# Splitting a group norm's last aggregate, moving its chain, and a new ending for a window-attention and convolution kernel

## The chip, the cores and the metric

One core of a Trainium2 chip runs the whole program. The metric is the device time of one execution in microseconds, the median of several runs. The engines are named as in the profile: PE (TensorE matmul), PEld (its weight loads), DVE (VectorE), ACT (ScalarE), POOL (GpSimd) and SP (SyncE, which here only issues DMAs). Each engine works through its own queue of instructions in order and waits for the others by semaphores.

## The reference

The input `x` is 2 images of 128 channels x 256 x 256, fp32. Two layers follow, each a residual around a group norm (32 groups of 4 channels, statistics over the whole image).

```python
# layer 0: windows of 8x8 queries, keys and values from 12x12 around them, 4 heads of 32
x = x + L0(_gn(x))
    qkv = einsum('bchw,oc->bohw', x, W_qkv)
    attn = q*SCALE @ k.T + rel_pos_emb(q) + FIXED_MASK   # mask: only every second row and column
    out = softmax(attn) @ v                              # then W_out
# layer 1: three convolutions, no activation
x = x + L1(_gn(x))
    t1 = conv(x, w1)          # 5x1 along the height, 128 -> 128 channels
    t3 = conv(t1, w3)         # 3x1 along the height, depthwise
    t4 = unfold3_dil2(x) * w4 # 3 taps of distance 2 along the width, 128 -> 8 channels
    y  = t4 * t3              # the 8 channels repeated 16 times
```

The mask leaves only pairs of pixels whose row and column offsets have one parity, so a window splits into four classes (row parity, column parity) of 16 queries and 36 keys.

## The kernel before

Channels lie on the 128 partitions. An image is cut into 32 strips of 8 rows, `k` counts the 64 strips of both images (`NB` = 2, `NS` = 32). Two generator-like stages run one after the other and overlap a little at their border.

**Set-up** (L226 to L254). 32 loads of 8 rows (1 MB) of image 0 go through six buffers, and `Norms.chunk` (L117) makes one `bn_stats` of 512 columns for every two rows: 128 in all. Then `Norms.steps` (L123) is run to its end inside `normalise(0)`: one `bn_aggr` over all 768 statistics (L127), a matmul with an averaging matrix that puts the mean over 4 channels (L130), mean and variance on DVE, a second such matmul (L141), square root on ACT (L147), and five small DVE operations for the reciprocal and one for the negated mean.

**Layer 0** (`attention_fast`, from L165). The order on every engine is the program's order (`manual_schedule`), so each call below stands in the queues of all engines at the place where it is written. The unit `u` is half a strip (a row parity `r`); there are 128. In a unit: at `r == 0` the next strip is normalised (`normalise`, DVE L322, L327, L328 and POOL L313); `input_stats` makes four `bn_stats` of the second image while the first is worked on, mostly in odd units and in units 4 and 8; `by_place` (POOL L337) sorts the next strip's pixels; `biases` (L458) and `scores` (L474) fill the four PSUM banks `s0` to `s3`; ACT takes the exponential (L483); `values` (L439) makes four PSUM tiles that ACT and DVE copy out half each (L445); `coefficients` (L418) for the next strip; `attend` (L499) with its division on DVE (L505, L506); `turn`, the transposes on DVE (L517); keys (L354) in even units, queries (L393) in odd ones; `result_stats`, two `bn_stats` of the unit before; `project` (L354, DVE L533), which adds the residual and stores x1 to DRAM (SP L537). All PSUM tiles but the scores' come from one ring of four banks, `ps_pj`: a tile's matmul waits until the tile four before it has been read.

The group norm of the second image (`x1`) is spread over unit 61, that of the first image's result (`y0`) over unit 69: `norm_at` names the unit and the seven calls of `step()` in the loop each run one piece of `Norms.steps`. The norm of the second image's result (`y1`) is run in pieces in strips 3 to 7 of layer 1. In unit 8 DVE forms the six sums of convolution weights (`Weights.sums`, L641 to L644).

**Layer 1** (`convolutions_fast`, a generator). Its first pieces (loads, normalisation, row sums, unfold of strip 0) are called by `next(layer1)` in the last units of layer 0. Then per strip: `unfold(k)` (four matmuls L740, two ACT copies L750 and L751, five small DMAs L754 that shift pixels), `first_rows(k)`, two calls of `vertical` (the 5x1 convolution with shared sums: matmuls L760 and L799, ACT copy L794, DVE L803, L810, L816, and ACT L821, the first tap of the 3x1 convolution), `depthwise` (the other two taps, DVE L828), `spread` (four matmuls L839 that repeat the 8 channels) into the score banks, and `combine` (DVE L849), the product. `finish` adds the residual by a DMA of POOL that accumulates (L857), and one strip later `store` writes the result. The last strip adds the residual itself, half on POOL (L870, L871), half on DVE (L873), and stores in two halves.

Tiles come from pools whose memory is a stack: the pools of layer 1 (`f_t1`, `f_wk1`) are opened after those of layer 0 are closed and reuse their memory; `f_both`, `f_raw` and the PSUM pools live through both layers.

Of the kernel before, what the change touches and what calls it, by code (L numbers as in the profile page):

```python
# [20 lines left out]
P = 128  # L21
W = 256
# [84 lines left out]
class Norms:  # L107


    def __init__(self, nc, glob, small, gavg, ns):  # L110
        self.nc, self.glob, self.small, self.gavg, self.ns = nc, glob, small, gavg, ns
        self.done = {}

# [8 lines left out]

    def steps(self, st, ps_pool, name, tag="pj"):  # L123

        nc, glob, small, gavg = self.nc, self.glob, self.small, self.gavg
        mv = small.tile([P, 2], F32, tag="mv", name=f"mv_{name}")
        nc.vector.bn_aggr(mv, st.rearrange("p n k -> p (n k)"))  # L127
        yield
        pm = ps_pool.tile([P, 512], F32, tag=tag, name=f"pm_{name}")
        nc.tensor.matmul(pm[:, 0:1], gavg, mv[:, 0:1], start=True, stop=True)  # L130
        yield
        mean = glob.tile([P, 1], F32, tag=f"mean_{name}", name=f"mean_{name}")
        nc.vector.tensor_copy(mean, pm[:, 0:1])
        d = small.tile([P, 1], F32, tag="d", name=f"d_{name}")
        nc.vector.tensor_sub(d, mv[:, 0:1], mean)
        q = small.tile([P, 1], F32, tag="q", name=f"q_{name}")
        nc.vector.tensor_mul(q, d, d)
        nc.vector.tensor_add(q, q, mv[:, 1:2])
        yield
        pv = ps_pool.tile([P, 512], F32, tag=tag, name=f"pv_{name}")  # L140
        nc.tensor.matmul(pv[:, 0:1], gavg, q, start=True, stop=True)  # L141
        yield
        v = small.tile([P, 1], F32, tag="v", name=f"v_{name}")
        nc.vector.tensor_scalar(v, pv[:, 0:1], 1e-5, None, ALU.add)
# [23 lines left out]
def attention_fast(tc, io, x1_d, norm, st_x, st_y, tags, ends, weights, both, layer1):  # L168
# [6 lines left out]
    with ExitStack() as l0:  # L175
# [49 lines left out]
        with ExitStack() as setup:  # L225
# [35 lines left out]

        stats_at, norm_at = {}, {}
        for b in range(NB - 1):
            for s in range(NS - 2):
                stats_at[2 * (b * NS + s) + 1] = b + 1, s
            stats_at[2 * (b * NS + 2)] = b + 1, NS - 1
            stats_at[2 * (b * NS + 4)] = b + 1, NS - 2
            norm_at[2 * (b * NS + NS - 2) + 1] = st_x, b + 1, f"x{b + 1}"
            norm_at[2 * ((b + 1) * NS + 2) + 1] = st_y, b, f"y{b}"
        coming, sxs = sorted(stats_at), {}  # L270

        def load_next():
            if coming:
                u = coming.pop(0)
                b, s = stats_at[u]
                sxs[u] = t = rawp.tile([P, 8, W], F32, tag="sx", name=f"f_sx_{b}_{s}", bufs=1)
                nc.sync.dma_start(t, x[b, :, 8 * s : 8 * s + 8, :])

        def input_stats(u):
            b, s = stats_at[u]  # L280
            norm.chunk(st_x[b], 4 * s, sxs.pop(u))

# [270 lines left out]
        with tc.manual_schedule(engines=ORDERED):  # L553
# [7 lines left out]
            for u in range(NU):  # L561
# [35 lines left out]
                attend(u)  # L597
                step()
                if not later:
# [23 lines left out]
class Weights:  # L623
# [14 lines left out]
    def sums(self):  # L638

        w = [self.w1[:, i] for i in range(5)]  # L640
        self.nc.vector.tensor_add(self.w1s[:, 0], w[1], w[3])  # L641
        self.nc.vector.tensor_scalar(self.w1s[:, 1], w[3], -1.0, None, ALU.mult)
        for i, (a, b) in enumerate(((2, 1), (4, 3), (0, 1), (2, 3))):
            self.nc.vector.tensor_sub(self.w1s[:, 2 + i], w[a], w[b])  # L644


def convolutions_fast(tc, io, x1_d, norm, st_y, out, weights, count_good, both):
# [4 lines left out]
    with ExitStack() as l1:  # L652
# [11 lines left out]
        def load_rows1(b, s):  # L664

            if s == 0:
                pre = rawp.tile([P, 8, W], F32, tag="sx", name=f"raw1_{b}_pre", bufs=1)
                nc.sync.dma_start(pre[:, 5:8, :], x1_d[b][0][:, 0:3, :])
# [66 lines left out]
        def unfold(k):  # L735
# [26 lines left out]

        def first_rows(k):

            s = k % NS
            xt = xn[k % 2]
            t3 = wk.tile([P, 8, W], F32, tag="t3", name=f"t3_{k}")
# [4 lines left out]
            if s == 0:  # L772
                nc.gpsimd.memset(t1[:, 0:1, :], 0.0)
                top = taps(
                    f"{k}_first", 1,
                    [(w1[:, tap], xt[:, tap - 1 : tap, 2 : 2 + W]) for tap in (2, 3, 4)],
                )
                nc.scalar.copy(t1[:, 1:2, :], top)
            else:
                nc.scalar.copy(t1[:, 0:2, :], t1s[k - 1][:, 8:10, :])  # L780
            if s + 1 == NS:
                nc.gpsimd.memset(t1[:, 9:10, :], 0.0)

        def vertical(k, m, between=None):
# [13 lines left out]
            for i, w in enumerate((w1[:, 1], w1s[:, 1])):  # L798
# [18 lines left out]
                t1[:, 2 * m - 1 : 2 * m + 2 * n - 2 : 2, :], pa[:, 0:n], c[:, 0:n], ALU.add  # L817
            )
            t3 = ts[k][1]
            j = 2 * m - 4  # L820
# [43 lines left out]

        def finish_half(k, half):

            b, s = divmod(k, NS)
            t4, t3, y = ts[k]
            if half == 0:
                nc.gpsimd.tensor_tensor(y[:, 0:3, :], y[:, 0:3, :], raws[b, s - 1][:, 5:8, :], ALU.add)  # L870
                nc.gpsimd.tensor_tensor(y[:, 3:4, :], y[:, 3:4, :], raws[b, s][:, 0:1, :], ALU.add)  # L871
            else:
                nc.vector.tensor_tensor(y[:, 4:8, :], y[:, 4:8, :], raws[b, s][:, 1:5, :], ALU.add)  # L873
            nc.sync.dma_start(
                out[b, :, 8 * s + 4 * half : 8 * s + 4 * half + 4, :], y[:, 4 * half : 4 * half + 4]
            )

# [8 lines left out]
        yield  # L886
        unfold(0)
        yield

        tp = l1.enter_context(tc.tile_pool(name="f_t1", bufs=2))  # L890
        wk = l1.enter_context(tc.tile_pool(name="f_wk1", bufs=2))
        with tc.manual_schedule(engines=ORDERED):
            rows_buffer(1)
            for k in range(NB * NS):
                more = k + 1 < NB * NS
                if k + 2 < NB * NS:
                    load_rows1(*divmod(k + 2, NS))
                if k > 0:
                    unfold(k)
                first_rows(k)  # L900

# [18 lines left out]
                if not more:  # L920
                    finish_half(k, 0)
                depthwise(k, 4)
                combine(k, banks, (2, 3))
                if more:
                    finish(k)
                else:
                    finish_half(k, 1)

# [614 lines left out]
```

## Time and profile before

| what | value |
|---|---|
| three runs | 3078.32, 3076.55, 3078.05 us; median 3078.05 |
| the profiled execution | 3077.89 us, of it 3076.0 us span |
| mean granted TensorE clock | 0.998 |
| PE busy | 2950.9 us (96%) |
| DVE busy | 2522.4 us (82%) |
| ACT busy | 1732.8 us (56%) |
| POOL busy | 657.8 us (21%) |
| HBM read, written | 284.59 MB, 134.22 MB |

The span is the time from the first to the last instruction of the profiled execution; the runs' times hold also what lies around it. In lines of the timeline the columns are the start in us, the duration, engine, line, operation, output and inputs, how many instructions are merged into the line, and in brackets the engine's idle time ahead of it with what ended it. In lines of waits they are the waiting engine and line, what it waited for, the total in us, how often, and the longest.

### The profile page before, as it was taken

The numbers are of one execution on the slowest core, as the hardware profiler recorded it, in microseconds if no ns is written. First come the engines' busy times: TensorE is split into PE (matmuls) and PEld (weight loads), VectorE is DVE, ScalarE is ACT, GpSimd is POOL, SyncE is SP. The second block draws the span as 40 slices with busy tenths as digits, with TensorE's granted clock in tenths as the row PEclk, the third lists the DMA queues.
The fourth block names the chain that finished last, engine by engine and source line by source line (L and its number), as shares of the span: only waits on it lengthen the run. The fifth ranks groups of instructions, "written<-read, shape, count | busy, mean of one in ns | idle before, by whom it ended". The sixth has DMA issues, their size and how long they took to land.

```text
span 3076.0 us, 116627 instructions
## 1 busy us (share of the span) xinstructions
PE 2950.9 (96%) x52090; PEld 2223.8 (72%) x52090; DVE 2522.4 (82%) x4092; ACT 1732.8 (56%) x2673; POOL 657.8 (21%) x1433
## 2 busy tenths in 40 slices
PE   0799999999999999999999999999999999999998
PEld 0688888888888888888888888884444444444443
DVE  8788888888888877777777777768999999999998
ACT  0455555555555655555555555555666665666664
POOL 2322232323232222323232323220000000000001
PEclk9999999999999999999999999999999999999999
DMA  9433333333333221222222222225788888888886
GB/s 393 167 126 126 114 117 113 116 113 116 112 117 113 85 72 65 89 72 90 73 90 73 90 72 89 73 96 141 209 222 221 215 210 217 216 217 216 217 216 167
DMA packets 137404, 434.78 MB, mean 141 GB/s; under 512 B 12992, under 2 KB 87616, under 8 KB 104384
## 3 DMA queue, kind: packets, MB, share of 16 engines
q1 hardware_dynamic: 127824, 361.18, 33.8%
q0 software_dynamic: 9072, 66.06, 11.7%
q8 instruction: 412, 6.75, 0.9%
q14 instruction: 96, 0.79, 0.1%
HBM read 284.59 MB, written 134.22 MB: 136 GB/s over the span
## 4 chain that ended last, share of the span: by engine, by line
PE 93%; DVE 2%; ACT 1%; issue 0%; POOL 0%; DMA 0%; SPq 0%; DVEq 0%; ACTq 0%
PE f_pv L439 15%; PE a_e L760 10%; PE a_o L760 10%; PE f_s L474 8%; PE f_o L499 8%; PE f_pk L354 8%; PE f_pq L393 7%; PE f_py L354 7%; PE f_pa L418 4%; PE f_s L458 4%; PE a_d L799 3%; PE b L839 2%; PE a_c L760 2%; PE g L740 2%; POOL f_xq L337 0%
## 5 line engine op out<-in xcount | busy, mean ns | idle before, releaser
L445 DVE COPY f_vt<-f_pv 64x512 f32<-64x512 f32 x512 | 354.2, 695 | 299.5 <-ACT f_vt L445 299.3
L337 POOL COPY f_xq<-f_xn 128x128 f32<-128x128 f32 x1024 | 399.2, 441 | 707.9 <-DVE f_xn L322 647.9
L439 PE MATMUL f_pv<-f_wqkvT,f_xn 128*128 128x128 f32 x4096 | 491.3, 278 | 0.0
L439 PEld LDWEIGHTS f_pv<-f_wqkvT,f_xn 128*128 128x128 f32 x4096 | 466.9, 192 | 8.6
L483 ACT ACTIVATE f_p<-f_s 128x512 f32<-128x512 f32 x512 | 264.5, 602 | 320.0 <-PE f_s L474 320.0
L399 ACT ACTIVATE f_q<-f_pq,f_head 128x512 f32<-128x512 f32 x512 | 303.1, 703 | 145.2 <-PE f_pq L393 145.2
L445 ACT COPY f_vt<-f_pv 64x512 f32<-64x512 f32 x512 | 298.2, 584 | 116.9 <-PE f_pv L439 116.5
L821 ACT ACTIVATE t<-t,w 128x1024 f32<-128x1024 f32 x128 | 146.9, 1148 | 372.4 <-DVE t L816 367.9
L828 DVE SCALAR_TENSOR_TENSOR t<-t,w,t 128x1024 f32<-128x1024 f32 x256 | 329.9, 1288 | 7.4 <-ACT t L821 1.3
L474 PEld LDWEIGHTS f_s<-f_q,f_kt 64*64 64x64 f32 x16384 | 250.9, 135 | 50.1 <-issue 49.9
L474 PE MATMUL f_s<-f_q,f_kt 64*64 64x64 f32 x16384 | 268.7, 220 | 0.6 <-issue 0.6
L367 ACT COPY f_kt<-f_pk 128x512 f32<-128x512 f32 x256 | 154.6, 604 | 196.4 <-PE f_pk L354 196.4
L499 PE MATMUL f_o<-f_vt,f_p 128*32 128x66 f32 x16384 | 263.6, 222 | 1.4 <-issue 0.7
L857 POOL DMA_DIRECT2D y<-f_x x63 | 54.7, 868 | 915.2 <-DVE y L849 900.2
L499 PEld LDWEIGHTS f_o<-f_vt,f_p 128*32 128x32 f32 x16384 | 241.9, 110 | 10.8 <-DVE f_cf L431 1.0
L354 PE MATMUL f_py<-f_ot,f_woT 128*128 128x256 f32 x1024 | 242.2, 379 | 2.2 <-DVE f_ot L517 2.2
L354 PE MATMUL f_pk<-f_xn,f_wqkvT 128*128 128x256 f32 (+2 forms) x1258 | 243.0, 345 | 0.0
L393 PE MATMUL f_pq<-f_xq,f_wq_s 128*128 128x256 f32 (+1 forms) x1370 | 240.5, 331 | 0.8 <-DVE f_rc L505 0.8
L313 POOL COPY f_xn<-f_xn 128x1280 f32<-128x1280 f32 x62 | 86.7, 1399 | 720.6 <-PE f_pv L439 720.6
L760 PE MATMUL a_e<-xm,w1s 128*128 128x512 f32 x512 | 240.7, 591 | 0.0
L760 PE MATMUL a_o<-xm,w1s 128*128 128x512 f32 x512 | 240.3, 590 | 0.0
L393 PEld LDWEIGHTS f_pq<-f_xq,f_wq_s 128*128 128x128 f32 x1370 | 208.2, 191 | 23.3 <-PE pv_x L141 0.4
(131 smaller groups left out, 4696.9 us busy)
## 6 DMA issues: line engine op xcount, KB each, us to landing
f_raw<-in_x SPq DMA_DIRECT2D x62, 1280.0 KB, 7.8
f_sx<-in_x SPq DMA_DIRECT2D x64, 1024.0 KB, 12.4
f_x<-f_x SPq DMA_DIRECT2D x128, 512.0 KB, 3.4
y<-f_x POOLq DMA_DIRECT2D x63, 1024.0 KB, 8.0
out<-y SPq DMA_DIRECT2D x63, 1024.0 KB, 4.4
raw<-f_x SPq DMA_DIRECT2D x64, 640.0 KB, 6.4
raw<-f_x SPq DMA_DIRECT2D x62, 384.0 KB, 6.5
t<-t4p SPq DMA_DIRECT2D x192, 32.0 KB, 4.7
```

The costliest lines, as they stand in the source:

```text
L337: nc.gpsimd.tensor_copy(xq[:, half, t2, :, :, c].rearrange("p t r n e -> p r t n e"), cells[:, :, 16 * half + c : 16 * half + 16 : 2, 1 + ...
L354: nc.tensor.matmul(dst[:, 512 * lo // last : 512 * hi // last], w, moving[:, n * lo // last : n * hi // last], start=True, stop=True,)
L367: nc.scalar.copy(cur[:, c, 1:129, 2:6], pk.rearrange("p (j i) -> p j i", i=4))
L393: nc.tensor.matmul(pq.rearrange("p (h n e t) -> p h t n e", h=2, n=8, e=2)[:, half, lo:hi], wq_s, xq[:, half, :, :, r, c].rearrange("p s t ...
L399: nc.scalar.activation(q[:, c, :, i], pq.rearrange("p (n x) -> p n x", n=NPAIR), AF.Copy, scale=head[:, i : i + 1],)
L439: nc.tensor.matmul(pv[:, P * n : P * n + P], xn[k % 2][:, r, 4 * j + n].rearrange("p c x -> p (c x)"), wvT, start=True, stop=True,)
L445: (nc.vector.tensor_copy if c else nc.scalar.copy)(vt[rows, 4 * j : 4 * j + 4, :, c, 0:32], pv[rows].rearrange("p (n h d) -> p n h d", n=4 ...
L474: nc.tensor.matmul(sc[g][n // 8][64 * c : 64 * c + 64, n % 8].rearrange("p i x -> p (i x)"), keys_k[rows, c, 48 * n : 48 * n + 64], qs[u][ ...
L483: nc.scalar.activation(pts[u][:, g, 8 * half : 8 * half + 8].rearrange("p n i x -> p (n i x)"), sc[g][half].rearrange("p n i x -> p (n i x ...
L499: nc.tensor.matmul(po[32 * h : 32 * h + 32, n - lo], p[:, h // 2, n, h % 2], vt[:, n, h], start=True, stop=True,)
L760: nc.tensor.matmul(pa[:, : n * W], w, rows, start=i == 0, stop=i == len(terms) - 1)
L828: nc.vector.scalar_tensor_tensor(t3[:, j : j + 4], t1[:, j + tap : j + tap + 4, :], w3[:, tap : tap + 1], t3[:, j : j + 4], ALU.mult, ALU.add,
```

## The change

- **Aggregate in quarters.** A new `quarter` runs `bn_aggr` over a quarter of the statistics; `steps` takes the four means and variances and combines them (with `last=True` it makes the fourth quarter itself, with `last=False` all four have been made). In the set-up the quarters stand between the loads; for `x1`, `y0` and `y1` they are placed at the end of chosen even units (`quarter_at`).
- **Statistics of the second image.** 30 loads in odd units only: eight of 10 rows, then 22 of 8 rows. Units 4 and 8 have none.
- **Chain of the norm.** The `step()` calls move within units 61 and 69: two after `scores`, two after `values`, one ahead of `attend`, one after `turn`.
- **Weight sums** on POOL instead of DVE.
- **Keys** of the second image's first strip, part 0: one matmul of 512 columns instead of two of 256.
- **Memory:** `f_wk` is opened ahead of `f_x1`; the statistics tile has 10 rows; the first strip's `t4` uses rows of another tile.
- **First-row taps** of strip 0 are issued with the unfold, inside the last unit of layer 0.
- **Last strip:** its order is new, and the 3x1 convolution of its lower four rows is made by TensorE with three diagonal matrices, made in strip 60 (one load, three ACT operations). POOL has no part in it any more.

```diff
-    def steps(self, st, ps_pool, name, tag="pj"):
+    def quarter(self, st, name, i):
+        if i == 0:
+            self.mvs[name] = self.glob.tile([P, 4, 2], F32, tag=f"mv_{name}", name=f"mv_{name}")
+        self.nc.vector.bn_aggr(
+            self.mvs[name][:, i], st[:, self.ns * i : self.ns * i + self.ns].rearrange("p n k -> p (n k)")
+        )
+
+    def steps(self, st, ps_pool, name, tag="pj", last=True):
-        mv = small.tile([P, 2], F32, tag="mv", name=f"mv_{name}")
-        nc.vector.bn_aggr(mv, st.rearrange("p n k -> p (n k)"))
-        yield
+        if last:
+            self.quarter(st, name, 3)
+            yield
+        mv = self.mvs[name]
...
-        nc.tensor.matmul(pm[:, 0:1], gavg, mv[:, 0:1], start=True, stop=True)
+        nc.tensor.matmul(pm[:, 0:4], gavg, mv[:, :, 0], start=True, stop=True)
...
-        nc.vector.tensor_copy(mean, pm[:, 0:1])
-        d = small.tile([P, 1], F32, tag="d", name=f"d_{name}")
-        nc.vector.tensor_sub(d, mv[:, 0:1], mean)
+        nc.vector.tensor_reduce(mean, pm[:, 0:4], AX.X, ALU.add)
+        nc.vector.tensor_scalar(mean, mean, 0.25, None, ALU.mult)
+        d = small.tile([P, 4], F32, tag="d", name=f"d_{name}")
+        nc.vector.tensor_scalar(d, mv[:, :, 0], mean, None, ALU.subtract)
+        nc.vector.tensor_mul(d, d, d)
+        nc.vector.tensor_add(d, d, mv[:, :, 1])
         q = small.tile([P, 1], F32, tag="q", name=f"q_{name}")
-        nc.vector.tensor_mul(q, d, d)
-        nc.vector.tensor_add(q, q, mv[:, 1:2])
+        nc.vector.tensor_reduce(q, d, AX.X, ALU.add)
...
                 norm.chunk(st_x[0], 4 * s, t)
+                if s % 8 == 7 and s < 31:
+                    norm.quarter(st_x[0], "x0", s // 8)
+        wk = l0.enter_context(tc.tile_pool(name="f_wk", bufs=2))
         x1p = l0.enter_context(tc.tile_pool(name="f_x1", bufs=2))
-        wk = l0.enter_context(tc.tile_pool(name="f_wk", bufs=2))
...
-            for s in range(NS - 2):
-                stats_at[2 * (b * NS + s) + 1] = b + 1, s
-            stats_at[2 * (b * NS + 2)] = b + 1, NS - 1
-            stats_at[2 * (b * NS + 4)] = b + 1, NS - 2
+            row = 0
+            for i in range(NS - 2):
+                n = 10 if i < 8 else 8
+                stats_at[2 * (b * NS + i) + 1] = b + 1, row, n
+                row += n
+            for i, u in enumerate((30, 46, 58, 60)):
+                quarter_at[2 * b * NS + u] = st_x, b + 1, f"x{b + 1}", i
...
+        for b in range(NB):
+            for i, u in enumerate((34, 50, 66, 68) if b + 1 < NB else (34, 42, 50)):
+                quarter_at[2 * b * NS + u] = st_y, b, f"y{b}", i
...
-                    steps = norm.steps(st[i], ps_pj, name)
+                    steps = norm.steps(st[i], ps_pj, name, last=False)
...
-                step()
                 if more:
                     by_place(k + 1, (2 * r, 2 * r + 1))
...
                 scores(u)
+                step()
+                step()
                 for j in range(4):
                     values(u, j)
                 step()
+                step()
                 if more:
                     coefficients(k + 1, r)
...
                 step()
                 attend(u)
-                step()
...
                 turn(u)
                 step()
...
-                        emit(keys(u + 2, TWO if top else THREE))
+                        emit(keys(u + 2, ONE if u > 0 and top and s else TWO if top else THREE))
...
-                step()
                 if u > 0:
                     result_stats(u - 1)
                 project(u)
-                step()
+                if u in quarter_at:
+                    st, i, name, part = quarter_at[u]
+                    norm.quarter(st[i], name, part)
...
-        self.nc.vector.tensor_add(self.w1s[:, 0], w[1], w[3])
+        self.nc.gpsimd.tensor_add(self.w1s[:, 0], w[1], w[3])
...
-                t4 = both.sb.tile([P, 2, W], F32, tag="t4", name=f"t4_{k}")
+                t4 = raws[0, -1][:, 0:2, :]
...
+        def diagonals():
+            ident = wk.tile([P, P], F32, tag="ident", name="ident1", bufs=1)
+            nc.sync.dma_start(ident, io["c_ident"])
+            dg = wk.tile([P, 3, P], F32, tag="dg", name="dg", bufs=1)
+            for tap in range(3):
+                nc.scalar.activation(dg[:, tap], ident, AF.Copy, scale=w3[:, tap : tap + 1])
+            return dg
...
+        def last_strip(k, dg):
...
+            banks = spread(k)
+            combine(k, banks, (0, 1))
+            spreads = wk.tile([P, 2, 512], F32, tag="spreads", name="spreads", bufs=1)
+            for j in range(2):
+                nc.scalar.copy(spreads[:, j], banks[2 + j])
+            vertical(k, 4)
+            residual(0, 3, raws[b, s - 1][:, 5:8, :])
+            residual(3, 4, raws[b, s][:, 0:1, :])
+            save(0, 4)
+            for j in range(2):
+                lo = 4 + 2 * j
+                pd = ps_pj.tile([P, 512], F32, tag="pj", name=f"d_{k}_{j}")
+                for tap in range(3):
+                    nc.tensor.matmul(
+                        pd, dg[:, tap], t1s[k][:, lo + tap : lo + tap + 2, :].rearrange("p r w -> p (r w)"),
+                        start=tap == 0, stop=tap == 2,
+                    )
+                nc.vector.tensor_tensor(
+                    y[:, lo : lo + 2, :].rearrange("p r w -> p (r w)"), pd, spreads[:, j], ALU.mult
+                )
+                residual(lo, lo + 2, raws[b, s][:, lo - 3 : lo - 1, :])
+                save(lo, lo + 2)
...
         unfold(0)
+        top = top_row(0)
         yield
...
+                if k + 4 == NB * NS:
+                    dg = diagonals()
...
                 depthwise(k, 2)
-                vertical(k, 4)
+                if more:
+                    vertical(k, 4)
                 if k > 0:
                     store(k - 1)
+                if not more:
+                    last_strip(k, dg)
+                    break
```

In `last_strip`, `residual` is a DVE addition of the rows of x1 onto `y`, and `save` a store by SP. `vertical(k, 4)` returns in the last strip ahead of its ACT operation L821. `top_row(0)` holds the three taps that `first_rows(0)` issued before; `first_rows` copies its result.

More of the change, by code (lines that the diff above doesn't have):

```diff
@@ L111, in __init__ @@
         self.nc, self.glob, self.small, self.gavg, self.ns = nc, glob, small, gavg, ns
-        self.done = {}
+        self.done, self.mvs = {}, {}
     def new(self, name, tag):
@@ L143, in steps @@
         v = small.tile([P, 1], F32, tag="v", name=f"v_{name}")
-        nc.vector.tensor_scalar(v, pv[:, 0:1], 1e-5, None, ALU.add)
+        nc.vector.tensor_scalar(v, pv[:, 0:1], 0.25, 1e-5, ALU.mult, ALU.add)
         yield
@@ L253, in attention_fast @@
                 norm.chunk(st_x[0], 4 * s, t)
+                if s % 8 == 7 and s < 31:
+                    norm.quarter(st_x[0], "x0", s // 8)
+        wk = l0.enter_context(tc.tile_pool(name="f_wk", bufs=2))
         x1p = l0.enter_context(tc.tile_pool(name="f_x1", bufs=2))
-        wk = l0.enter_context(tc.tile_pool(name="f_wk", bufs=2))
         raws, norms, qs, cfs, pts, ots, rcs, ons, x1s = ({} for _ in range(9))
         stats_at, norm_at = {}, {}
+        quarter_at = {}
         for b in range(NB - 1):
-            for s in range(NS - 2):
-                stats_at[2 * (b * NS + s) + 1] = b + 1, s
-            stats_at[2 * (b * NS + 2)] = b + 1, NS - 1
-            stats_at[2 * (b * NS + 4)] = b + 1, NS - 2
+            row = 0
[5 more added lines that the diff above has]
+                quarter_at[2 * b * NS + u] = st_x, b + 1, f"x{b + 1}", i
             norm_at[2 * (b * NS + NS - 2) + 1] = st_x, b + 1, f"x{b + 1}"
             norm_at[2 * ((b + 1) * NS + 2) + 1] = st_y, b, f"y{b}"
+        for b in range(NB):
+            for i, u in enumerate((34, 50, 66, 68) if b + 1 < NB else (34, 42, 50)):
+                quarter_at[2 * b * NS + u] = st_y, b, f"y{b}", i
         coming, sxs = sorted(stats_at), {}
@@ L274, in load_next @@
                 u = coming.pop(0)
-                b, s = stats_at[u]
-                sxs[u] = t = rawp.tile([P, 8, W], F32, tag="sx", name=f"f_sx_{b}_{s}", bufs=1)
-                nc.sync.dma_start(t, x[b, :, 8 * s : 8 * s + 8, :])
+                b, row, n = stats_at[u]
+                t = rawp.tile([P, 10, W], F32, tag="sx", name=f"f_sx_{b}_{row}", bufs=1)
+                sxs[u] = t[:, 0:n]
+                nc.sync.dma_start(sxs[u], x[b, :, row : row + n, :])
         def input_stats(u):
-            b, s = stats_at[u]
-            norm.chunk(st_x[b], 4 * s, sxs.pop(u))
+            b, row, n = stats_at[u]
+            norm.chunk(st_x[b], row // 2, sxs.pop(u))
         def load_rows(k):
@@ L640, in sums @@
         w = [self.w1[:, i] for i in range(5)]
-        self.nc.vector.tensor_add(self.w1s[:, 0], w[1], w[3])
-        self.nc.vector.tensor_scalar(self.w1s[:, 1], w[3], -1.0, None, ALU.mult)
+        self.nc.gpsimd.tensor_add(self.w1s[:, 0], w[1], w[3])
+        self.nc.gpsimd.tensor_scalar(self.w1s[:, 1], w[3], -1.0, None, ALU.mult)
         for i, (a, b) in enumerate(((2, 1), (4, 3), (0, 1), (2, 3))):
-            self.nc.vector.tensor_sub(self.w1s[:, 2 + i], w[a], w[b])
+            self.nc.gpsimd.tensor_sub(self.w1s[:, 2 + i], w[a], w[b])
 def convolutions_fast(tc, io, x1_d, norm, st_y, out, weights, count_good, both):
@@ L666, in load_rows1 @@
             if s == 0:
-                pre = rawp.tile([P, 8, W], F32, tag="sx", name=f"raw1_{b}_pre", bufs=1)
+                pre = rawp.tile([P, 10, W], F32, tag="sx", name=f"raw1_{b}_pre", bufs=1)
                 nc.sync.dma_start(pre[:, 5:8, :], x1_d[b][0][:, 0:3, :])
@@ L761, in taps, with top_row, first_rows @@
             return pa[:, : n * W].rearrange("p (r w) -> p r w", w=W)
-        def first_rows(k):
+        def top_row(k):
+            xt = xn[k % 2]
+            return taps(
+                f"{k}_first", 1,
+                [(w1[:, tap], xt[:, tap - 1 : tap, 2 : 2 + W]) for tap in (2, 3, 4)],
+            )
+        def first_rows(k, top=None):
             s = k % NS
-            xt = xn[k % 2]
             t3 = wk.tile([P, 8, W], F32, tag="t3", name=f"t3_{k}")
@@ L773, in first_rows @@
                 nc.gpsimd.memset(t1[:, 0:1, :], 0.0)
[L774 to L778, printed above, removed]
+                nc.scalar.copy(t1[:, 1:2, :], top_row(k) if top is None else top)
             else:
@@ L818, in vertical @@
             )
+            if m == 4 and k + 1 == NB * NS:
+                return
             t3 = ts[k][1]
@@ L863, in store, with residual, save @@
             nc.sync.dma_start(out[b, :, 8 * s : 8 * s + 8, :], done.pop(k))
-        def finish_half(k, half):
+        def last_strip(k, dg):
             b, s = divmod(k, NS)
[L868 to L876, printed above, removed]
+            y = ts[k][2]
+            def residual(lo, hi, rows):
+                nc.vector.tensor_tensor(y[:, lo:hi, :], y[:, lo:hi, :], rows, ALU.add)
+            def save(lo, hi):
+                nc.sync.dma_start(out[b, :, 8 * s + lo : 8 * s + hi, :], y[:, lo:hi])
+            banks = spread(k)
[17 more added lines that the diff above has]
+                    y[:, lo : lo + 2, :].rearrange("p r w -> p (r w)"), pd, spreads[:, j], ALU.mult
+                )
+                residual(lo, lo + 2, raws[b, s][:, lo - 3 : lo - 1, :])
+                save(lo, lo + 2)
         load_rows1(0, 0)
@@ L897, in convolutions_fast @@
                     load_rows1(*divmod(k + 2, NS))
+                if k + 4 == NB * NS:
+                    dg = diagonals()
                 if k > 0:
                     unfold(k)
-                first_rows(k)
+                first_rows(k, top if k == 0 else None)
                 vertical(k, 2, (lambda: start_strip(k + 1)) if more else None)
@@ L913, in convolutions_fast @@
                 depthwise(k, 2)
-                vertical(k, 4)
+                if more:
+                    vertical(k, 4)
                 if k > 0:
                     store(k - 1)
+                if not more:
+                    last_strip(k, dg)
+                    break
                 banks = spread(k)
                 combine(k, banks, (0, 1))
-                if not more:
-                    finish_half(k, 0)
                 depthwise(k, 4)
                 combine(k, banks, (2, 3))
[L924 to L927, printed above, removed]
+                finish(k)
 class Both(NamedTuple):
```

## The prediction

> **What bounds the kernel now.** I read the page first (shares, chain of waits), then who waited for whom on PE, and then the timeline where PE stands still.
>
> ```profile
> PE 2950.9 (96%) x52090; PEld 2223.8 (72%) x52090; DVE 2522.4 (82%) x4092; ACT 1732.8 (56%) x2673; POOL 657.8 (21%) x1433
> PE 93%; DVE 2%; ACT 1%; issue 0%; POOL 0%; DMA 0%; SPq 0%; DVEq 0%; ACTq 0%
> ```
>
> TensorE sets the time: 93% of the chain. Only 3076.0 - 2950.9 = 125 us are PE idle, so a change that takes no work from PE can only win in these, and around a few stalls.
>
> ```profile
> PE pm_x L130 <- issue: 86.9, 1, 86.9
> PE f_pa L418 <- DVE f_vt L445: 5.3, 4, 2.9
> PE a_c L760 <- DVE c L803: 2.2, 2, 1.3
> ```
>
> The 86.9 us are the set-up, in which batch 0 is read for its statistics; the rest are single places. To find their full price I took, from the timeline, the start of the bias matmuls (L458) in each of the 128 attention units, and of the spread matmuls (L839) in each of the 64 strips of layer 1. A unit takes 15.33 us and a strip 15.17, to 0.03, except here (excess): unit 4 0.84, unit 8 4.56, unit 61 1.54, unit 62 2.76, unit 64 0.90, unit 69 1.53, unit 70 1.22; strip 0 1.67, strip 1 0.31, strip 3 1.97, strip 31 1.30. Units 62 and 64 hold the two top-key steps of the second image (0.90 of real matmuls each), and strip 31 its first-row taps (1.29); these stay. Unit 8:
>
> ```profile
> 239.43 2.46 DVE L119 BATCH_NORM_STATS2 st_x<-f_sx 128x6 f32<-128x512 f32 x4
> 242.35 1.71 DVE L644 TENSOR_TENSOR w1s<-w 128x128 f32<-128x128 f32 x4
> 244.09 2.52 DVE L445 COPY f_vt<-f_pv 64x512 f32<-64x512 f32 x4
> 244.93 1.88 PE L418 MATMUL f_pa<-f_xq,f_wb 128*64 128x64 f32 x32 [2.95 <-DVE f_vt L445]
> ```
>
> VectorE does four statistics and six weight sums ahead of its value copies; PE waits 2.95 us for a PSUM bank, then runs at half clock for about 3.4 us (granted clock 0.50 from 246 to 248; these matmuls take 1.88 instead of 1.15). That is the 4.56.
>
> [...] L828 takes 2.64 us instead of 1.28 beside POOL's additions. [...] The trace has 1283 ns for each; the square root moves, its two loads remain.
>
> **The change part by part.**
>
> *Set-up.* The last of 128 statistics ends at 89.86.
>
> ```profile
> 89.90 3.62 DVE L127 BATCH_NORM_AGGREGATE mv_x<-f_st_x 128x2 f32<-128x768 f32 x1
> 20.00:75.00 55.00, 0.00 (x0) 0.00 (x0) 54.08 (x89) 2.68 (x14) 0.00 (x0) 1.00 1.01 419
> ```
>
> The second line (a window; the last three columns are clock, DMA share, GB/s) shows the DMA full at 419 GB/s, and loads land 12.4 us after issue, five loads deep. So the loads pace, not VectorE: it has about 0.1 us of wait per 1 MB load. A quarter aggregate is not in the trace. [...] It can't gain beyond 0.90, a quarter of the whole. Three quarters lie between loads; of the last of them 8 x 0.1 is caught up in the eight loads that follow, 0.15 is left. At the end 0.96 instead of 3.62; the mean and variance step has six small operations for four (+0.45 at 0.16 to 0.2 us each). Gain 3.62 - 0.96 - 0.15 - 0.45 = **2.05**.
>
> *Statistics of batch 1 and weight sums.* Units 4 and 8 lose their four statistics (0.84 and 4.56 with the sums): **5.4**. The first eight odd units get a fifth, 0.6 us; in unit 7 VectorE waits 1.76 us for ACT before its first value copy, so it is covered; without that cover 0.6 x 8 = 5. The six sums stand in POOL's queue at unit 8 ahead of the place copies (L337), on which PE's coefficient matmuls (L418) wait. POOL waits 10 us there for the normalisation; at 0.44 us (its copies of 128) to 1.70 (its slowest addition) six need 2.6 to 10. Cost 0. The ten-row loads on SP are the same bytes in 30 issues for 32.
>
> *Chain in units 61 and 69.* The whole aggregate leaves the start of the unit; the quarters (0.96) sit at the end of units 30 to 68, where VectorE then waits 1.8 to 4 us in the next unit. The mean step comes after the scores, so PE no longer runs into it (waits of 0.3 and 0.4 in each unit). The two small matmuls stay, about 0.3. Gain 1.54 + 1.53 - 2 x 0.33 = **2.4**. The last step (six operations, 1.1 us) is now ahead of the statistics and projection additions of the same unit on VectorE, which is late there already, so the next normalisation starts about 1 us late instead of 2.2. Units 62 and 70: 2.76 - 0.90 + 1.22 = 3.08, less 0.4 each = **2.3**. The return to the exponential's table still delays unit 62's first exponential by 1.28, which ACT made good by the value copies before.
>
> *One-part keys.* Only unit 62 takes that branch: four matmul records of 256 become two of 512. 4 x 0.22 against 2 x 0.43: **0**.
>
> *Start of layer 1.*
>
> ```profile
> 2083.24 1.96 PE L354 MATMUL f_py<-f_ot,f_woT 128*128 128x256 f32 x8 [1.47 <-DVE f_ot L517]
> 2085.04 1.46 PE L760 MATMUL a_first<-xm,w 128*128 128x256 f32 x6
> 2091.25 0.37 ACT L794 COPY both<-a_c 128x256 f32<-128x256 f32 x1 [4.30 <-DMA f_x<-f_x]
> ```
>
> The first-row taps (1.29 from first start to next group) go into PE's wait of 1.47 for the transposes: -1.29. ACT's copy waits for the store of the last x1 tile, whose memory layer 1 reuses. It holds up the next normalisation and VectorE; that is strips 0 and 1 (1.67 + 0.31, of which 1.35 are visible PE waits). With x1 allocated behind the work pool, layer 1's pools (38 + 49 KB by the tile sizes) end before it (at some 95 KB): no such wait. Gain 1.29 + 1.8 = **3.1**. Freeing the t4 tile and the larger statistics tile only move addresses.
>
> *Strip 3.* The aggregate of 3.61 shrinks to 0.96, and VectorE waits about 0.6 for ACT there anyway; the mean matmul stays. 1.97 - 0.27 = **1.7**.
>
> *Diagonals, strip 60.* One 64 KB load on SP, three ACT scalings at 0.3. ACT is queued ahead of the unfold copies, but waits 5.5 us per strip for VectorE. **0**; up to 1.5 if the load lands late.
>
> *Last strip.*
>
> ```profile
> 3063.12 4.02 DVE L828 SCALAR_TENSOR_TENSOR t<-t,w,t 128x1024 f32<-128x1024 f32 x2
> 3063.29 2.77 POOL L870 TENSOR_TENSOR y<-y,raw 128x768 f32<-128x768 f32 x1 [9.40 <-DVE y L849]
> 3068.57 1.22 DVE L873 TENSOR_TENSOR y<-y,raw 128x1024 f32<-128x1024 f32 x1
> ```
>
> Now: PE ends at 3061.9, VectorE at 3069.8. After: spread moves ahead of the second vertical step. Its last small transfer lands at 3054.1 (issued 3052.1, 2.0 to land), PE wants it at 3054.4. PE: 3054.4 + 1.11 spread + 6.45 vertical + 12 x 0.43 diagonal taps = 3067.1. VectorE: product 0.7, addition 0.65, end 3068.6. The last store has half the bytes: its packets took 1.6 us, so -0.7. Gain 1.15 + 0.75 = **1.9**. SP gets three stores for two, apart in time.
>
> Sum: 2.05 + 5.4 + 2.4 + 2.3 + 3.1 + 1.7 + 1.9 = 18.85. Profiled execution: 3077.89 (span 3076.0 and 1.9 around it), 0.16 below the median of 3078.05, within the runs' spread. **3059.2 us.**
>
> **The rivals.**
> *B, the start of layer 1 does not move.* Another reader of the reused memory, or the store itself, takes the wait's place. For: the wait ends on a DMA, and the allocation isn't in the trace. Against: sizes. 3.1 lost: 3062.3.
> *C, the chain's stall only moves.* VectorE is late at the end of unit 61, where 1.1 us are now put ahead of the additions; 4.7 lost: 3063.9. With the tail gaining nothing as well (spread waits for its transfers), 3065.8.
> *D, the quarter is priced by instruction.* At 3.01: set-up lags 9 - 2.4 + 3.01 instead of 3.62, 8.5 worse than my sum, strip 3 loses 1.2: 3069. At 3.61: some 3075. It decides against the change as a whole at about 3.7.
> *E, slower: VectorE becomes the bound of layer 1.* It is busy 137.6 of 151.7 us over ten strips, slack 1.4 per strip. Small tiles change size (4 to 16 bytes, others new)[...]. It decides from 1.4 + 18.85/64 = 1.7 us a strip. [...]
>
> **How the numbers follow.** Forecast 61% (its own range 3056 to 3062), B 17%, C 12%, D 8%, E 2%. Low end: all excesses vanish and the tail gains 2.6: 3056. High end: D's bound, 3069. About 0.2% (6.2 us) is what a measurement of this kernel can tell from no change: below 3071.9 lie the forecast, B, C and most of D: 0.95; within 0.03; slower 0.02.
>
> **What would show it.** Pitch of units 4, 8, 69, 70 and strips 1, 3 at 15.33 and 15.17; unit 62 near 16.6; the aggregate at about 0.96; first normalisation near 95.1 instead of 97.2; no DMA wait before the copy at L794; last VectorE instruction 1.2 us after PE's last. Wrong if the aggregate takes 3 us, if PE waits at the moved spread, or if a strip is longer than 15.2.

## The result and the profile after

| | median us | lowest to highest | ratio to before, 95% interval |
|---|---|---|---|
| before | 3078.02 (6 runs) | 3076.55 to 3078.65 | |
| after | 3064.92 (6 runs) | 3063.96 to 3065.69 | 0.9958 [0.9946, 0.9970] |

The change gains 13.1 us; the forecast was 18.85 (3059.2). The time lies within the range, 5.7 us above the forecast. The profiled execution of after took 3064.28, of it 3062.5 span (before 3076.0).

The page of after, busy times and the shares of the chain of waits:

```profile
PE 2954.8 (96%) x52100; PEld 2224.4 (73%) x52100; DVE 2517.6 (82%) x4107; ACT 1732.8 (57%) x2677; POOL 654.4 (21%) x1437
PE 95%; DVE 0%; ACT 0%; POOL 0%; DMA 0%; issue 0%; SPq 0%; ACTq 0%
```

TensorE is busy 3.9 us longer and yet the span is 13.5 shorter; its idle time fell from 125 to 108. TensorE now holds 95% of the chain, VectorE none. Whom TensorE waited for:

```profile
PE pm_x L139 <- issue: 84.3, 1, 84.3
...
PE a_o L783 <- ACT t L774: 3.8, 1, 3.8
...
PE f_py L375 <- DVE f_ot L538: 0.9, 1, 0.9
```

The waits on the value copies (5.3) and on `c` (2.2) are gone, the wait of the first matmul for the set-up is 2.6 shorter, and one line is new: 3.8 us on ACT, once. The timeline of after, at the places that the prediction priced:

```profile
89.92 1.02 DVE L127 BATCH_NORM_AGGREGATE mv_x<-f_st_x 128x2 f32<-128x192 f32 x1
...
236.88 0.69 DVE L466 COPY f_vt<-f_pv 64x512 f32<-64x512 f32 x1 [0.50 <-ACT f_vt L466]
...
238.78 1.15 PE L439 MATMUL f_pa<-f_xq,f_wb 128*64 128x64 f32 x32
...
2069.20 1.56 PE L783 MATMUL a_first<-xm,w 128*128 128x256 f32 x6
2070.74 1.97 PE L375 MATMUL f_py<-f_ot,f_woT 128*128 128x256 f32 x8
...
2073.17 0.37 ACT L829 COPY both<-a_c 128x256 f32<-128x256 f32 x1 [1.95 <-PE a_c L783]
...
3050.12 5.31 PE L925 MATMUL d<-t,dg 128*128 128x512 f32 x12
...
3056.20 0.69 DVE L907 TENSOR_TENSOR y<-y,raw 128x512 f32<-128x512 f32 x1
```

The last aggregate takes 1.02 instead of 3.62. In unit 8 VectorE starts its value copies with time to spare and the coefficient matmuls run without a wait at full clock (1.15). The first-row taps stand in front of `f_py`, whose wait of 1.47 is gone. ACT's copy at the border waits for TensorE and no longer for a DMA. At the end VectorE's last operation ends 1.5 us after TensorE's last matmul.

The pitch of units and strips, read as in the prediction, gives each term. The excess of strip 60 is that of the stretch from the spread of strip 59 to the spread of strip 60. The third and fourth columns hold what was predicted and measured for the term.

| term of the sum | excess before, after | predicted | measured |
|---|---|---|---|
| set-up (start of unit 0 at 110.45, then 108.25; first pitch 0.12 shorter) | | 2.05 | 2.3 |
| units 4 and 8 | 0.84 and 4.56; none | 5.4 | 5.4 |
| units 61 and 69 | 1.54 and 1.53; 0.33 each | 2.4 | 2.4 |
| units 62 and 70 | 2.76 and 1.22; 1.44 and 0.14 | 2.3 | 2.4 |
| start of layer 1 (1.30 ahead of strip 0, 1.67 in it) | | 3.1 | 3.0 |
| strip 3 | 1.97; 0.22 | 1.7 | 1.75 |
| strip 6 | 0.39; none | | 0.4 |
| last strip (spread of strip 62 to the end: 30.40; 28.72) | | 1.9 | 1.7 |
| **diagonals, strip 60** | none; **5.77** | **0** | **-5.8** |

The rows add up to 13.55, the spans differ by 13.5. All the missing gain is in one row. Strip 60 in the timeline of after; the SPq lines are DMA issues:

```profile
2982.49 0.34 SPq L900 DMA_DIRECT2D out<-y  x1
2982.87 0.43 SPq L694 DMA_DIRECT2D raw<-f_x  x1
2983.35 0.92 SPq L696 DMA_DIRECT2D raw<-f_x  x1
2984.31 1.04 SPq L813 DMA_DIRECT2D ident<-in_c_ident  x1
...
2984.14 1.15 ACT L858 ACTIVATE t<-t,w 128x1024 f32<-128x1024 f32 x1 [5.53 <-DVE t L851]
2990.54 0.98 ACT L816 ACTIVATE dg<-ident,w 128x128 f32<-128x128 f32 x3 [5.25 <-DMA ident<-in_c_ident]
2991.43 0.56 ACT L773 COPY t4p<-g 128x512 f32<-128x512 f32 x1
2991.90 0.58 ACT L774 COPY t<-g 128x512 f32<-128x512 f32 x1
...
2992.53 3.22 PE L783 MATMUL a_o<-xm,w1s 128*128 128x512 f32 x4 [3.80 <-ACT t L774]
2995.54 1.53 PE L783 MATMUL a_o<-xm,w 128*128 128x512 f32 x2
```

SP issues the 64 KB identity behind a store of 1 MB and rows of 1 MB; it is usable 6.2 us after its issue. ACT reaches the scalings at 2985.29, stands for 5.25 us, and only then makes the unfold copies L773 and L774. These empty the PSUM bank that the `a_o` matmuls need: in the ring of four, their tile follows four places behind that of the unfold. TensorE stands 3.80 us and then runs slow: 3.22 and 1.53 us for what takes 1.88 and 1.02 elsewhere, another 1.85. Together 5.65 of the 5.77.

### The profile page after: what moved, and what is told of

It is laid out like the page before. It is cut to its first block, busy times and chain, and to the rows that moved or that the text cites. A ratio compares the mean times of both kernels' runs of the same rounds, so it can differ in the third digit from the quotient of the medians.

```text
span 3062.5 us, 116727 instructions
## 1 busy us (share of the span) xinstructions
PE 2954.8 (96%) x52100; PEld 2224.4 (73%) x52100; DVE 2517.6 (82%) x4107; ACT 1732.8 (57%) x2677; POOL 654.4 (21%) x1437
## 4 chain that ended last, share of the span: by engine, by line
PE 95%; DVE 0%; ACT 0%; POOL 0%; DMA 0%; issue 0%; SPq 0%; ACTq 0%
PE f_pv L460 16%; PE a_o L783 11%; PE a_e L783 11%; PE f_s L495 8%; PE f_o L520 8%; PE f_pq L414 8%; PE f_pk L375 8%; PE f_py L375 7%; PE f_pa L439 4%; PE f_s L479 4%; PE a_d L834 4%; PE b L876 2%; PE a_c L783 2%; PE g L763 2%; POOL f_xq L358 0%; DMA ident<-in_c_ident 0%
## 5 line engine op out<-in xcount | busy, mean ns | idle before, releaser
L858 ACT ACTIVATE t<-t,w 128x1024 f32<-128x1024 f32 x127 | 145.9, 1149 | 367.6 <-DVE t L851 362.8
L865 DVE SCALAR_TENSOR_TENSOR t<-t,w,t 128x1024 f32<-128x1024 f32 x254 | 325.8, 1283 | 7.4 <-ACT t L858 1.3
L375 PE MATMUL f_pk<-f_xn,f_wqkvT 128*128 128x128 f32 (+2 forms) x1256 | 244.2, 346 | 0.0
```

The lines of the kernel that those rows point to most:

```text
L375: nc.tensor.matmul(dst[:, 512 * lo // last : 512 * hi // last], w, moving[:, n * lo // last : n * hi // last], start=True, stop=True,)
L865: nc.vector.scalar_tensor_tensor(t3[:, j : j + 4], t1[:, j + tap : j + tap + 4, :], w3[:, tap : tap + 1], t3[:, j : j + 4], ALU.mult, ALU.add,
```

## The experiments

The question is strip 60: is the loss **ACT's queue** (the scalings wait, and the unfold copies stand behind them), is it the load's own slowness or SP's time, or does the new ending with its taps on TensorE simply cost more than was thought? And are the other rows right for the reasons given, or only in size? Experiment 3 takes up the last strip, experiments 6 to 9 the start of layer 1, unit 8 and the set-up. The rows of units 61 to 70, of strip 3 and of strip 6 were not taken apart by any experiment and rest on the traces.

**1. The load one strip earlier.** The scalings stay in strip 60; `identity` is the load, taken out of `diagonals`.

```diff
+                if k + 5 == NB * NS:
+                    ident = identity()
                 if k + 4 == NB * NS:
-                    dg = diagonals()
+                    dg = diagonals(ident)
```

> The changed kernel with the load of the identity matrix issued one strip earlier (strip 59), the three scalings left in strip 60. Theory W (the cost of strip 60 is ACT standing behind a load that lands late, and with it PE and its half clock): the excess of 5.77 us in strip 60 goes, PE has no wait at the a_o matmuls there, 3059.1 us. Rival A (the three scalings on ACT are themselves too much for the strip): the excess stays above 1 us, 3061 to 3065. The load itself is expected to take about 6 us to land again, since it stands behind the same transfers, but nobody waits.

Measured: 3059.16 us (3058.70 to 3059.31), ratio 0.9941 [0.9928, 0.9955], 5.8 below after. From the timeline of this run, ACT in strip 60 and the matmuls that waited before:

```profile
2985.69 0.97 ACT L820 ACTIVATE dg<-ident,w 128x128 f32<-128x128 f32 x3
...
2987.03 0.58 ACT L774 COPY t<-g 128x512 f32<-128x512 f32 x1
...
2989.06 1.88 PE L783 MATMUL a_o<-xm,w1s 128*128 128x512 f32 x4
```

No wait, no excess in strip 60, matmuls at full speed. This also gives the **slack**: ACT's copy ends at 2987.61, the matmuls start at 2989.06, so ACT may be 1.45 us later than here before TensorE stands. In after ACT waited 5.25, and 5.25 - 1.45 = 3.80, the wait of TensorE in that run.

**2. The load in strip 60, but ahead of the rows on SP's queue.**

```diff
+                if k + 4 == NB * NS:
+                    ident = wk.tile([P, P], F32, tag="ident", name="ident1", bufs=1)
+                    nc.sync.dma_start(ident, io["c_ident"])
                 if k + 2 < NB * NS:
                     load_rows1(*divmod(k + 2, NS))
                 if k + 4 == NB * NS:
-                    dg = diagonals()
+                    dg = diagonals(ident)
```

> The changed kernel with the load of the identity matrix issued in strip 60 ahead of the two row loads instead of behind them; scalings unchanged. Theory Q (the load lands late because 1 MB of row loads and a 1 MB store are ahead of it in the same queue): with 1 MB ahead it lands some 4.5 us after issue, ACT waits about 2.2 instead of 5.2, PE waits about 0.7 instead of 3.8 and keeps its full clock: about 5 us faster than the changed kernel, 3060. Rival S (the load is slow by itself, many packets of 512 bytes): it lands 6.2 us after an issue 1.5 us earlier, PE waits 2.3, 3061.5 to 3063.

Measured: 3060.95 us (3060.67 to 3061.29), ratio 0.9947 [0.9934, 0.9961]. The timeline of this run:

```profile
2982.93 0.34 SPq L898 DMA_DIRECT2D out<-y  x1
2983.31 0.43 SPq L954 DMA_DIRECT2D ident<-in_c_ident  x1
...
2987.56 0.99 ACT L814 ACTIVATE dg<-ident,w 128x128 f32<-128x128 f32 x3 [1.81 <-DMA ident<-in_c_ident]
...
2989.55 1.99 PE L783 MATMUL a_o<-xm,w1s 128*128 128x512 f32 x4 [0.36 <-ACT t L774]
```

With only the store ahead of it the load is usable 4.2 us after its issue, not 6.2: 2 us of its lateness come from its place behind the rows. From the start of the store's issue it is 4.63 here and 8.05 in after; the rows in between, their issue and their bytes, cost 3.4. What the load takes with nothing ahead of it was not run. ACT waits 1.81, TensorE 1.81 - 1.45 = 0.36, and keeps nearly its full speed (1.99 for 1.88). The 1.8 us over the first experiment are 0.63 in this strip, 0.82 in the next, where TensorE waits 0.45 for VectorE, and 0.46 behind the spread of strip 62; what the last comes from is not shown.

**3. The ending of before, in the changed kernel.** The diagonals and the whole new last strip are taken out, the old halves put back.

```diff
-                    last_strip(k, dg)
-                    break
...
+                if not more:
+                    finish_half(k, 0)
```

> The changed kernel with the last strip as it was before (no diagonals, POOL adds half of the residual, two stores), all else kept. If my sum holds, the diagonals cost 5.77 and the new ending gains 1.7: this kernel is 4.1 us faster than the changed one, 3060.8. If the loss in strip 60 is something else than the diagonals (addresses, the row loads), the excess stays and it is 1.7 us slower, 3066.6.

Measured: 3060.85 us (3060.76 to 3061.24), ratio 0.9947 [0.9933, 0.9961]; no excess in strip 60. The new ending as it was made costs 4.1 us: 5.8 lost in strip 60, 1.7 gained at the end. The ending itself is sound, as experiment 1 against this one says (3059.16 against 3060.85).

**4. The kernel before with the diagonals alone**, made and not used.

```diff
+                if k + 4 == NB * NS:
+                    dg = diagonals()
```

> The kernel before with only the diagonals added (load and three scalings in strip 60, their result unused). Theory W: 5.8 us slower than before, 3083.8, with an excess of 5.8 in strip 60 alone. Rival A or an effect of other parts of the change on strip 60: clearly less, 3078 to 3081.

Measured: 3083.81 us (3081.29 to 3085.85), ratio 1.0020 [1.0012, 1.0028] to 3077.58 of before beside it. The timeline of its profiled execution:

```profile
3008.43 0.98 ACT L790 ACTIVATE dg<-ident,w 128x128 f32<-128x128 f32 x3 [5.55 <-DMA ident<-in_c_ident]
...
3010.42 3.78 PE L760 MATMUL a_o<-xm,w1s 128*128 128x512 f32 x4 [4.10 <-ACT t L751]
3013.99 1.91 PE L760 MATMUL a_o<-xm,w 128*128 128x512 f32 x2
```

One load and three scalings lose 6.2 us without any of the rest of the change. Again 5.55 - 1.45 = 4.10. The slow stretch is longer here (3.78 and 1.91 for 1.88 and 1.02), the strip's excess 7.35. The profiled execution was one of the longer ones (3085.26), 1.45 above the median.

**5. The load where it was, the scalings one strip later.** This is the mirror of experiment 1: now ACT's side moves and SP's stays.

```diff
                 if k + 4 == NB * NS:
-                    dg = diagonals()
+                    ident = identity()
+                if k + 3 == NB * NS:
+                    dg = diagonals(ident)
```

> The changed kernel with its identity load where it was, in strip 60 behind the rows, and only the three scalings of ACT moved one strip on, to strip 61. Theory W (the loss of strip 60 is ACT standing 5.25 us in front of the scalings with the unfold copies queued behind it): no wait of ACT for the load, strip 60 without excess, 3059.2. Rival S (the load itself, 1 us of SP's time and 64 KB ahead of the pixel shifts on SP's queue, delays the strip, and the earlier load escaped that by its place): half or more of the excess stays, 3061 to 3065.

Measured: 3059.54 us (3059.29 to 3059.58), ratio 0.9941 [0.9927, 0.9954]. ACT's scalings at 3001.40 have no wait and strip 60 no excess. The time is 0.4 us over that of experiment 1, but none of it lies in strip 60: neither the load's bytes nor SP's microsecond costs anything there, only standing in ACT's queue does. Strip 60 is settled: four placements, one mechanism.

**6. The pools swapped back** in the kernel of experiment 1, to test the term of 3.1 at the start of layer 1.

```diff
-        wk = l0.enter_context(tc.tile_pool(name="f_wk", bufs=2))
         x1p = l0.enter_context(tc.tile_pool(name="f_x1", bufs=2))
+        wk = l0.enter_context(tc.tile_pool(name="f_wk", bufs=2))
```

> The kernel with the early identity load (3059.16 us), and the order of the two pools put back: x1's tiles ahead of the work tiles, so that layer 1's pools reach into their memory again. Theory M (the gain of 3.0 us at the start of layer 1 is the wait for the store of the last x1 tile, plus 1.3 for the first-row taps in the gap): ACT's copy at the first row group waits for a DMA again, the taps' 1.3 stay gained, strips 0 and 1 together come out 1.7 to 2.0 us longer, time 3060.9 to 3061.2. Rival R (the taps taken into the gap, with the unfold, are the whole gain; the store has landed by then or is hidden): no wait that counts, 3059.2.

Measured: 3061.81 us (3061.56 to 3062.17), ratio 0.9948 [0.9935, 0.9962], 2.65 over experiment 1. The timeline of this run at the border:

```profile
2074.82 0.58 SPq L558 DMA_DIRECT2D f_x<-f_x  x1
...
2079.20 0.37 ACT L833 COPY both<-a_c 128x256 f32<-128x256 f32 x1 [7.78 <-DMA f_x<-f_x]
...
2090.30 0.70 PE L783 MATMUL a_c<-sm,w1s 128*128 128x256 f32 x2 [1.58 <-DVE c L842]
```

The wait for the store of x1 is back, longer than the 4.30 of before. The mechanism is the one named, but its size is above what theory M expected (3061.2 at most). From unit 127 to the spread of strip 0 takes 27.80 us (26.98 in after), from there to strip 1 17.20 (15.17): 2.85 for the order of the pools. The whole term is 2.97. So with the pools as before, the taps moved forward gain only 0.1 of it: the store lands when it lands (ACT's copy starts 20.2 us after the start of unit 127 in before, 20.4 here), and TensorE only comes sooner to the matmuls behind that copy. The split in the prediction, 1.3 for the taps and 1.8 for the wait, does not hold when the taps come first. The other order, the pools alone with the taps where they were, was not run.

**7. The six weight sums back on VectorE**, in the kernel of experiment 1, the statistics left out of unit 8.

```diff
-        self.nc.gpsimd.tensor_add(self.w1s[:, 0], w[1], w[3])
+        self.nc.vector.tensor_add(self.w1s[:, 0], w[1], w[3])
...
-            self.nc.gpsimd.tensor_sub(self.w1s[:, 2 + i], w[a], w[b])
+            self.nc.vector.tensor_sub(self.w1s[:, 2 + i], w[a], w[b])
```

> The kernel with the early identity load (3059.16 us), and the six weight sums of unit 8 back on VectorE; the four statistics stay out of that unit. Theory H (PE's loss is the wait plus a stretch at half clock[...]): VectorE is 1.7 us late instead of 4.2, PE waits under 1 us and keeps its clock, unit 8 is 0 to 1 us longer, time 3059.2 to 3060.2. Rival L (the loss goes with the work put ahead of the copies, 4.56 x 1.71/4.17 = 1.9): 3061. Rival N (the six sums alone bring nearly the whole loss, and GpSimd has the gain of unit 8): 3063.5.

Measured: 3060.31 us (3059.82 to 3060.41), ratio 0.9943 [0.9930, 0.9957], 1.15 over experiment 1. The timeline of this run, unit 8:

```profile
239.04 2.52 DVE L466 COPY f_vt<-f_pv 64x512 f32<-64x512 f32 x4
...
239.88 1.15 PE L439 MATMUL f_pa<-f_xq,f_wb 128*64 128x64 f32 x32 [0.83 <-DVE f_vt L466]
```

TensorE waits 0.83 and runs on at full clock (1.15; the mean granted clock of the run is 1.0); the unit is 0.91 longer. Theory H's range holds for the unit (0 to 1); the time is 0.1 over its 3060.2. VectorE is later than theory H had counted (it took four of the six sums only). The loss does not go with the work put ahead of the copies: 4.66 us of it in before (239.43 to 244.09) cost 4.56, 2.54 here (236.50 to 239.04) cost 0.91. What the statistics cost without the sums can be read in before, where unit 4 has four statistics and no sums:

```profile
177.25 2.46 DVE L119 BATCH_NORM_STATS2 st_x<-f_sx 128x6 f32<-128x512 f32 x4
179.74 2.52 DVE L445 COPY f_vt<-f_pv 64x512 f32<-64x512 f32 x4
180.58 1.15 PE L418 MATMUL f_pa<-f_xq,f_wb 128*64 128x64 f32 x32 [0.75 <-DVE f_vt L445]
```

Here 2.49 us of work make TensorE wait 0.75 and cost 0.84. In all three cases the wait is the work less about 1.7 us (1.74, 1.71, 1.71): a slack again. Statistics alone cost 0.84, sums alone 0.91, both together 4.56. The slack is spent only once, and behind the wait of 2.95 the half clock (0.50 for 3.41 us) came on top. So neither work is the large part of unit 8's loss; an estimate from these figures is that taking out either one wins about 3.7 of the 4.56.

**8. and 9. The quarters of the set-up at its end.** First by writing them there, in the kernel of experiment 1:

```diff
-                if s % 8 == 7 and s < 31:
-                    norm.quarter(st_x[0], "x0", s // 8)
...
     def group(self, st, ps_pool, name):
+        for i in range(3):
+            self.quarter(st, name, i)
```

> The kernel with the early identity load (3059.16 us), and image 0's first three quarters made at the end of the set-up, with the fourth, instead of between the loads; nothing of the arithmetic changes. Theory P (the loads set the pace of the set-up and hide the three quarters there): the first normalisation starts 3 x 1.02 = 3.1 us later, less the 0.1 to 0.2 that the last quarter between loads left over, time 3062.1 to 3062.3; dearer than one aggregate over all 768 columns (3.62) by 0.4. Rival V (VectorE sets the pace of the set-up, so that work only changes its place): 3059.2.

Measured: 3059.03 us (3058.74 to 3059.23), ratio 0.9940 [0.9926, 0.9953]. That looks like rival V, but the statement was not tested: the list of operations on this tile shows the four aggregates of the set-up, `f_st_x`, still spread out.

```profile
L127 DVE BATCH_NORM_AGGREGATE mv_x<-f_st_x x4: 1021/1022/1022, 29.4 to 89.9; 128x2 f32<-128x192 f32 x4
```

The set-up's order is not the written one (only the two layers are): a quarter whose statistics are complete is put between the loads by itself. So the statistics were dealt out so that every quarter needs the last load:

```diff
-                norm.chunk(st_x[0], 4 * s, t)
-                if s % 8 == 7 and s < 31:
-                    norm.quarter(st_x[0], "x0", s // 8)
+                norm.chunk(st_x[0], s, t, NS)
+                if s == 31:
+                    for i in range(3):
+                        norm.quarter(st_x[0], "x0", i)
```

> The kernel with the early identity load (3059.16 us), in which the four statistics of a load of image 0 are written one into each quarter instead of all into one, so that every quarter hangs on the last load and all four aggregates must stand behind it, whatever order is written. Theory P (the loads set the pace of the set-up and hide three quarters between them): the first normalisation starts 3 x 1.02 = 3.06 us later less 0.1 to 0.2, time 3062.0 to 3062.3. Rival V (VectorE sets the pace of the set-up, work only changes its place): 3059.2.

Measured: 3061.65 us (3061.42 to 3062.38), ratio 0.9948 [0.9934, 0.9961], 2.5 over experiment 1. The timeline:

```profile
89.89 3.64 DVE L127 BATCH_NORM_AGGREGATE mv_x<-f_st_x 128x2 f32<-128x192 f32 x4
...
97.64 0.92 DVE L344 TENSOR_SCALAR f_xn<-f_raw,mean_x,rstd_x 128x640 f32<-128x640 f32 x1
```

Theory P holds: the last statistics end at 90.0 here and in experiment 1, the first normalisation starts at 97.64 instead of 95.14. The size is 0.5 below what was expected, because four aggregates in a row take 0.91 each, not 1.02. So the loads hide the three quarters between them.

## Why the prediction was right and where it failed

**Right.** The method, excess of each unit and strip over the common pitch, placed the gain: seven of its terms hold within 0.3 us. The aggregate came out at 1.02, which refutes rival D. The 0.96 of the prediction and rival D's 3.01, from which the upper end of 3069 comes, were the author's estimates: how much of the 3.62 us is fixed was not shown by any line of before. No DMA wait remains at the copy (rival B), TensorE has no new wait in units 61 and 69 (rival C), and all undisturbed strips keep 15.17 us (rival E, for whose loss no line of before gave a size). The 1283 ns in the prediction are the mean of ACT's eight table loads in before. GpSimd's six sums took 2.7 us (225.0 to 227.7) and GpSimd then still waited 7.3 us, as the prediction's lower bound had it. Two readings of the prediction are off without weight. Of the two operations L828 that it takes as beside GpSimd's additions, only the second took 2.64 us; the first, begun at 3063.12 ahead of the addition at 3063.29, took 1.28. And rival D's figures above 3.01 (3075 at 3.61, the turn at 3.7) do not come out of its own terms, four aggregates in the set-up and one in strip 3, which give about 3072 at 3.61.

**Failed: "Diagonals, strip 60 ... 0; up to 1.5 if the load lands late".** The step gave as its cover that ACT "waits 5.5 us per strip for VectorE". That wait is real (5.53 in the lines above), but it stands one instruction ahead of the scalings. ACT comes out of it, makes L858 and then is as busy as TensorE allows: what was free behind the scalings was 1.45 us, not 5.5. The bound of 1.5 was not worked out from any line. The prediction said that the unfold copies are queued behind, but not who waits for those, which is TensorE through the bank. The landing time is missing as well: the prediction has that of a small transfer of the last strip, 2.0 us, but none for this load, and leaves out what SP has queued in front in every strip. This load, issued by SP behind others, has 6.2 in after and 4.2 in experiment 2, which is 2 us less with 1 MB less ahead. Put in afterwards, ACT's measured 5.25 less 1.45, with the half clock priced as for unit 8 (1.6), makes the row -5.4 and the sum 3064.6, against the 3064.92 measured.

**Right in sum, not in what a part gains alone: the start of layer 1.** 3.1 was predicted and 3.0 measured, 1.30 of it ahead of strip 0 and 1.67 in it. But with the pools as before the taps gain 0.1, and the pools then 2.85: the 1.3 of the taps come in only when the wait for the store is gone. **Right, though not through the order of the source: the set-up.** The quarters lie between the loads and are hidden there, as stated (experiment 9); that the source puts them there made no difference in experiment 8. **Right in size, not tested:** the rows of units 61 to 70 and of strip 3. Strip 6 gained 0.4 that the prediction had not seen.

## What to carry to other kernels

A wait of an engine covers new work only if it stands behind that work in the queue; ACT's 5.53 us stood ahead of the scalings and covered nothing of their 5.25. Find the instruction after the insertion on whose result the critical engine waits, and measure how early that result is today. A small constant is loaded a stage before it is needed, and its landing is priced with the bytes already queued in front of it: 64 KB were usable after 6.2 us behind 2 MB and after 4.2 us behind 1 MB. Parts that remove waits from one place need not add: at the start of layer 1 the taps alone gave 0.1, and in unit 8 two works that cost 0.84 and 0.91 apart cost 4.56 together. Take each away alone before you book it.

## What had not been expected of the hardware

- **Half clock after a short stand.** In the traces of before and after the changes of the granted clock lie whole multiples of 3.41 us apart (42, 1 and 825 of them in before; 847, 1 and 18 in after). TensorE waits of 0.36, 0.83 and 1.58 us (experiments 2, 7 and 6) were followed by matmuls at or near their full pace (1.99 for 1.88, 1.15, and 0.59 from the third group on) and cost at most 0.5 more than themselves; the one of 1.47 in before left the clock at 1.00. Those of 2.95 (before) and 3.80 (after) were followed by one window of 3.41 us at 0.50, the one of 4.10 (experiment 4) by two (below); the slow matmuls cost about 1.6, 1.85 and 3.2 us on top of the waits. The windows of 3.41 us just ahead of the drop still held 0.46 us (before) and 0.61 us (after) of TensorE's work, so here 2.95 us of standing were enough; how short a wait can be and still bring the half clock is not shown. In experiment 4 the wait, up to 3010.42, reached 0.8 us into the next window, which stood at half clock, and so did the one behind it:

```profile
3006.21:3009.62 3.41, 0.11 (x1) 0.00 (x0) 0.71 (x2) 1.19 (x4) 0.86 (x1) 1.00 0.76 186
3009.62:3013.03 3.41, 2.61 (x3) 1.18 (x4) 1.38 (x2) 3.41 (x6) 0.00 (x0) 0.50 0.95 192
3013.03:3016.45 3.42, 3.42 (x6) 1.67 (x5) 0.50 (x1) 3.00 (x2) 0.00 (x0) 0.50 0.51 115
```

The columns are the window, its length, TensorE's busy time, that of PEld, DVE, ACT and POOL, the granted clock, the DMA's share and GB/s.
- **An aggregate has almost no fixed cost.** Over 768 columns it takes 3.62 us (before), four over 192 in a row 3.64 (experiment 9), a single one 1.02 (after), which is 0.11 more than one of the four.
